# Attention maxima from columns to rows: four transposes per pair of heads, or a trip through DRAM

## The chip, the cores and the metric

The kernel runs on one NeuronCore of a Trainium2 chip. The metric is the device time of one execution in microseconds (us), as the median of several runs. One further execution was recorded by the hardware profiler; all readings of the profile come from it.

## The reference, cut to what matters

The input is `x` of shape (4, 128, 64, 64): four images, 128 channels, 4096 positions. A first layer is attention with four heads of 32 channels over the 4096 positions, followed by an output projection, the residual and a layer norm. A second layer adds a 3x3 convolution, a spectral branch and a selective scan (Mamba). The change is in the attention:

```python
Q = split_heads(x_flat @ Wq + bq)
K = split_heads(x_flat @ Wk + bk)
V = split_heads(x_flat @ Wv + bv)
attn = jax.nn.softmax(jnp.einsum('bhnd,bhmd->bhnm', Q, K) * scale, axis=-1)
out = jnp.einsum('bhnm,bhmd->bhnd', attn, V)
```

For each query the softmax takes off the largest of its 4096 scores before the exponential.

## The kernel before

**Halves and steps.** Queries are handled in chunks of 512 (`L`), and heads in pairs. A chunk with a pair is a "half", `H`; there are 32 chunks x 2 pairs = 64 halves. The keys of a half are walked through in 32 (`NT`) steps. A loop over a step counter `t` writes the whole program out in order, for all engines. In step `t` it issues

- `scores_for_exp` (L494): keys as weights, queries as the moving operand, so that the scores stand with keys on partitions and queries along the row. Each score is the sum of three matmuls per head: query high part, query low part (both against a K tile that holds high and low rows), and a matmul of `sel` with `MX[H]`, which subtracts the query's maximum. ScalarE then takes the exponential (L502).
- `scores_for_max` (L454), seven steps ahead (`LEAD = 7`) and for the half that comes next: here 128 queries are the weights and 512 keys move, so that queries stand on partitions. VectorE reduces them to a maximum for each query and block of keys (L461, tile `part`). The step number `s` gives the block of keys `m` and the group of queries `t`.
- `times_values` (L514): the exponentials of the step before, times the values, accumulated over the half.
- parts of the scan (L827 to L873) on ScalarE, VectorE and GpSimd, and one load of `bc` (L810) by SyncE's queue about every four steps.

The two heads of a pair lie on partitions 0 to 63 and 64 to 127, so their matmuls use the two halves of the array's rows and run as pairs.

**The other work** (projections, norm, convolution, gates, output, the chain for the maxima) is written as generators. A planner (`Plan`) resumes each once its time has come and the places that it asks for are free in this step: `"P"` TensorE, `"D"` VectorE, `"A"` ScalarE, `"B"` one of two PSUM banks, and `""` for nothing, which only ends the step. The order that results is fixed when the program is built; every engine and SyncE's DMA queue work through their instructions in that order and wait on semaphores.

**The maxima.** `maxima(H)` starts at `H * NT - LEAD`, when the last scores for maxima of that half are out. It reduces `part` to one maximum for each query and head (L467), splits the negative into a high and a low part (L469, L471), copies and writes them into two columns of each 64-wide half of the tile `wide` (L470, L471), has TensorE transpose `wide` in four pieces of 128 x 128 into a PSUM bank (L476), and has ScalarE copy the result to `MX[H]` (L482). There the maxima stand in rows 0 and 32 (`HD`) of each 64-row half, with the queries along the row; all other rows are zero. `wide` is zeroed once, at the start.

SyncE's queue also carries the K and V tiles (L385, L394), the queries (L434), the inputs (L336), and a chain through DRAM that normalises each half (`zd` L541, `zc` L546, `rd` L551, `rz` L554).

Of the kernel before, what the change touches and what calls it, by code (L numbers as in the profile page):

```python
# [9 lines left out]
F32 = mybir.dt.float32  # L10
F32R = mybir.dt.float32r
AF = mybir.ActivationFunctionType
ALU = mybir.AluOpType
AX = mybir.AxisListType
# [3 lines left out]
P = 128  # L18
W = 64
HEADS = 4  # L20
HD = P // HEADS
PAIRS = HEADS // 2
HS = P // 2
L = 512
RPC = L // W
TPC = L // P
# [135 lines left out]
def attention_then_conv_mamba(  # L162
# [17 lines left out]
    nc = tc.nc  # L180
    ctx.enter_context(tc.manual_schedule())
    B, C, N = x.shape
    NCH = N // L
# [5 lines left out]
    const = ctx.enter_context(tc.tile_pool(name="const", bufs=1))  # L189
    att = ctx.enter_context(tc.tile_pool(name="att", bufs=2))  # L190
    loc = ctx.enter_context(tc.tile_pool(name="loc", bufs=2))
    dram = ctx.enter_context(tc.tile_pool(name="dram", bufs=2, space=DRAM))
# [8 lines left out]
    for h in range(HEADS):  # L201
        k, j = divmod(h, 2)
# [3 lines left out]
    for h in range(HEADS):  # L206
        k, j = divmod(h, 2)
# [9 lines left out]
    for h in range(HEADS):  # L217
        k, j = divmod(h, 2)
# [39 lines left out]
    ident = cst[:, K_ID : K_ID + P]  # L258
# [57 lines left out]
    ]  # L316
    VA = [const.tile([P, TPC, HEADS, HD + 1], F32, name=f"V_{i}") for i in range(NCH)]

    wide = const.tile([P, TPC, 2, HS], F32, name="wide")
    nc.gpsimd.memset(wide, 0.0)  # L320
    state = const.tile([P, NH * NS], F32, name="state")
    carry = const.tile([P, NH, TAPS - 1], F32, name="carry")

    rows = [slice(j * HS, (j + 1) * HS) for j in range(2)]
    used = [slice(j * HS, j * HS + HD + 1) for j in range(2)]

    plan = Plan(2, {"x": 2, "f": 1})

    def bank_tile(bank, shape, name):
        return psum.tile(shape, F32, tag=f"m{bank}", name=name)  # L330
# [66 lines left out]
    QT, MX = {}, {}  # L397
# [42 lines left out]
    part = {}  # L440

    def scores_for_max(H, s):

        k = H % PAIRS
        m, t = divmod(s, TPC)
        assert have["K", k, m] == H // PAIRS // NCH
        if s == 0:
            part[H] = att.tile([P, TPC, 2, NCH], F32, tag="part", name=f"part_{H}")

        tag = "s2" if H == 0 and s % 2 else "s1"  # L450
        sc = psum.tile([P, 2, L], F32, tag=tag, name=f"s1_{H}_{s}")
        for n in range(2):
            for j in range(2):
                nc.tensor.matmul(  # L454
                    sc[:, j, :],
                    QT[H][rows[j], n, t * P : (t + 1) * P],
                    KK[k][m][rows[j], :],
                    start=n == 0,
                    stop=n == 1,
                )  # L460
        nc.vector.tensor_reduce(part[H][:, t, :, m], sc, AX.X, ALU.max)  # L461

    def maxima(H):

        yield "D"
        mx = att.tile([P, TPC, 2], F32, tag="mx", name=f"mx_{H}")
        nc.vector.tensor_reduce(mx, part.pop(H), AX.X, ALU.max)  # L467
        hi = att.tile([P, TPC, 2], F32R, tag="mhi", name=f"mhi_{H}")
        nc.vector.tensor_scalar(hi, mx, -1.0, None, ALU.mult)  # L469
        nc.vector.tensor_copy(wide[:, :, :, 0], hi)  # L470
        nc.vector.scalar_tensor_tensor(wide[:, :, :, HD], mx, -1.0, hi, ALU.mult, ALU.subtract)  # L471
        yield ""
        bank = yield "PB"
        pm = bank_tile(bank, [P, L], f"pm_{H}")
        for t in range(TPC):
            nc.tensor.transpose(  # L476
                pm[:, t * P : (t + 1) * P], wide[:, t].rearrange("p j d -> p (j d)"), ident
            )
        yield "A"
        plan.release(bank)  # L480
        MX[H] = att.tile([P, L], F32R, tag="MX", name=f"MX_{H}")
        nc.scalar.activation(MX[H], pm, AF.Copy)  # L482

    es, po, oz = {}, {}, {}

# [555 lines left out]
    for H in range(HALVES):  # L1041
        if H % PAIRS == 0:
            plan.at((H - 1) * NT - LEAD - 30, 0, load_q(H // PAIRS))
            plan.at((H - 1) * NT - LEAD - 22, 0, project_q(H // PAIRS))
        plan.at((H - 1) * NT - LEAD - 8, 0, place_q(H))
        plan.at(H * NT - LEAD, 0, maxima(H))
        plan.at((H + 1) * NT + 1, 0, normalise(H, (H + 1) * NT + 12))
# [11 lines left out]
    t = 6 - SLOT  # L1059
    loaded = 0  # L1060
    end = (CHUNKS + 3) * SLOT
    while t < end or not plan.idle():
        H, m = divmod(t, NT)
# [3 lines left out]
        if 0 <= h1 + 1 < HALVES:  # L1067
            scores_for_max(h1 + 1, s1)
        H, m = divmod(t - 1, NT)
# [114 lines left out]
```

## Time and profile before

| what | us |
|---|---|
| median of three runs (6036.54 to 6038.84) | 6037.3 |
| the profiled execution, its own time | 6038.33 |
| its span, first to last instruction | 6036.5 |
| TensorE matmuls busy | 5847.1 |
| VectorE busy | 4360.0 |
| ScalarE busy | 3586.6 |
| GpSimd busy | 4482.6 |
| first scores for maxima | 63.2 |
| last exponential scores | 5813 |

In the lines of the profile, PE is TensorE, PEld its weight loads (they may overlap matmuls), DVE VectorE, ACT ScalarE, POOL GpSimd, and SP or SPq SyncE and its queue of DMAs. L454 is line 454 of the kernel before. A group's line has the engine, the operation, the tiles (`out<-in`), the shapes and the count; then the busy time and the mean duration in ns; then the time that the engine sat idle ahead of such instructions, and what ended it. TensorE's matmuls are pipelined, so durations overlap: the distance between the starts of two groups says what the first one cost.

### The profile page before, as it was taken

The numbers are of one execution on the slowest core, as the hardware profiler recorded it, in microseconds if no ns is written. First come the engines' busy times: TensorE is split into PE (matmuls) and PEld (weight loads), VectorE is DVE, ScalarE is ACT, GpSimd is POOL, SyncE is SP. The second block draws the span as 40 slices with busy tenths as digits, with TensorE's granted clock in tenths as the row PEclk, the third lists the DMA queues.
The fourth block names the chain that finished last, engine by engine and source line by source line (L and its number), as shares of the span: only waits on it lengthen the run. The fifth ranks groups of instructions, "written<-read, shape, count | busy, mean of one in ns | idle before, by whom it ended". The sixth has DMA issues, their size and how long they took to land. (4 is left out here: it accounts for less than half of the span.)

```text
span 6036.5 us, 82731 instructions
## 1 busy us (share of the span) xinstructions
PE 5847.1 (97%) x31382; PEld 2443.1 (40%) x31382; DVE 4360.0 (72%) x4569; ACT 3586.6 (59%) x4826; POOL 4482.6 (74%) x4522
## 2 busy tenths in 40 slices
PE   5999999999999999999999999999999999999976
PEld 2444444444444444444444444444444444444422
DVE  4557777777777777777777777777777777777657
ACT  1455666666666666666666666666666666666653
POOL 0006888778887778888788888777888887888877
PEclk7999999999999999999999999999999999999988
DMA  4012222224333223223432222322433222222233
GB/s 125 25 36 58 65 71 75 71 70 110 82 89 73 73 72 74 72 64 89 104 84 82 74 68 71 75 68 73 108 75 92 67 67 63 66 71 63 62 98 89
DMA packets 266641, 455.28 MB, mean 75 GB/s; under 512 B 46688, under 2 KB 48256, under 8 KB 266240
## 3 DMA queue, kind: packets, MB, share of 16 engines
q1 hardware_dynamic: 261584, 448.11, 28.1%
q8 instruction: 246, 4.03, 0.3%
q10 hardware_dynamic: 4656, 1.87, 0.1%
q14 instruction: 155, 1.27, 0.1%
HBM read 375.68 MB, written 65.80 MB: 73 GB/s over the span
## 5 line engine op out<-in xcount | busy, mean ns | idle before, releaser
L461 DVE TENSOR_REDUCE part<-s 128x2 f32<-128x1024 f32 x2048 | 2498.1, 1221 | 1411.4 <-PE s L454 1407.6
L502 ACT ACTIVATE e<-s 128x1024 f32<-128x1024 f32 x2048 | 2095.5, 1023 | 2121.6 <-PE s L494 2117.0
L514 PE MATMUL po<-e,V 128*33 128x512 f32 x8192 | 2180.9, 605 | 2.4 <-DVE oz L525 0.3
L494 PE MATMUL s<-Q,K 64*128 64x512 f32 x8192 | 1501.0, 444 | 13.5 <-ACT e L502 10.2
L454 PE MATMUL s<-K,Q 64*128 64x512 f32 x8192 | 1308.9, 397 | 41.4 <-DVE part L461 32.3
L854 POOL TENSOR_TENSOR hs<-hs,bc 128x512 f32<-128x512 f32 x948 | 1211.0, 1277 | 170.3 <-DVE hs L844 101.3
L494 PEld LDWEIGHTS s<-Q,K 64*128 64x128 f32 x8192 | 610.2, 185 | 1736.3 <-ACT e L502 1237.0
L832 POOL TENSOR_TENSOR db<-u,bc 128x512 f32<-128x512 f32 x948 | 1215.6, 1282 | 0.0
L873 POOL TENSOR_TENSOR acc<-acc,hs 128x512 f32<-128x512 f32 x894 | 1145.4, 1281 | 70.1
L844 DVE TENSOR_TENSOR_SCAN hs<-dA,state,db 128x512 f32<-128x512 f32 x826 | 1052.8, 1275 | 41.9 <-ACT dA L827 40.1
L454 PEld LDWEIGHTS s<-K,Q 64*128 64x128 f32 x8192 | 750.1, 185 | 294.9 <-DVE part L461 129.4
L494 PE MATMUL s<-MX,sel 64*128 64x512 f32 x4096 | 808.0, 391 | 0.0
L827 ACT ACTIVATE dA<-dt,negA 128x512 f32<-128x512 f32 x1024 | 703.2, 687 | 115.7 <-DVE V L844 69.5
L853 POOL COPY state<-hs 128x1 f32<-128x1 f32 x858 | 157.9, 184 | 789.8 <-DVE hs L844 786.0
L514 PEld LDWEIGHTS po<-e,V 128*33 128x33 f32 x8192 | 305.4, 109 | 886.5 <-issue 840.8
L494 PEld LDWEIGHTS s<-MX,sel 64*128 64x128 f32 x4096 | 383.9, 185 | 90.7
L928 PE MATMUL pf<-xp,cw 128*128 128x512 f32 x576 | 288.2, 618 | 0.0
L558 POOL TENSOR_TENSOR op<-op,rz 128x512 f32<-128x512 f32 x32 | 41.4, 1294 | 178.6 <-DMA rz<-rd 175.8
L844 DVE TENSOR_TENSOR_SCAN hs<-dA,zero,db 128x512 f32<-128x512 f32 x128 | 163.2, 1275 | 0.9 <-POOL db L832 0.7
L880 PE MATMUL acc<-V,cst 128*128 128x512 f32 x140 | 95.0, 783 | 63.6 <-POOL V L854 63.5
L928 PEld LDWEIGHTS pf<-xp,cw 128*128 128x128 f32 x576 | 96.8, 189 | 119.6 <-issue 117.9
L712 POOL TENSOR_TENSOR xs<-xs,sg_x 128x512 f32<-128x512 f32 x64 | 81.8, 1279 | 79.3 <-ACT sg_x L636 79.3
(147 smaller groups left out, 3571.2 us busy)
## 6 DMA issues: line engine op xcount, KB each, us to landing
bc<-bcd SPq DMA_DIRECT2D x487, 512.0 KB
Q<-qd SPq DMA_DIRECT2D x256, 128.0 KB
K<-kd SPq DMA_DIRECT2D x64, 256.0 KB
K<-bcd SPq DMA_DIRECT2D x42, 256.0 KB
vd<-vst SPq DMA_DIRECT2D x32, 264.0 KB
V<-vd SPq DMA_DIRECT2D x32, 264.0 KB
xq<-in_x SPq DMA_DIRECT2D x32, 256.0 KB
xk<-in_x SPq DMA_DIRECT2D x32, 256.0 KB
```

The costliest lines, as they stand in the source:

```text
L454: nc.tensor.matmul(sc[:, j, :], QT[H][rows[j], n, t * P : (t + 1) * P], KK[k][m][rows[j], :], start=n == 0, stop=n == 1,)
L461: nc.vector.tensor_reduce(part[H][:, t, :, m], sc, AX.X, ALU.max)
L494: nc.tensor.matmul(s[:, j, :], sel[rows[j], :] if n == 2 else KK[k][i][rows[j], t * P : (t + 1) * P], mov[rows[j], :], start=n == 0, stop= ...
L502: nc.scalar.activation(e, s, AF.Exp)
L514: nc.tensor.matmul(po[H][used[j], :], VA[i][:, t, 2 * k + j, :], e[:, j, :], start=m == 0, stop=m == NT - 1,)
L827: nc.scalar.activation(dA[c, v], dts[c][hf], AF.Exp, scale=negA[:, k : k + 1])
L832: engine.tensor_tensor(db[c, v], us[c][hf], bcs[c, n][0], ALU.mult)
L844: nc.vector.tensor_tensor_scan(hs, dA.pop((c, v)), db.pop((c, v)), state[:, k : k + 1] if c % NCH else zero, ALU.mult, ALU.add,)
L853: nc.gpsimd.tensor_copy(state[:, k : k + 1], hs[:, L - 1 :])
L854: nc.gpsimd.tensor_tensor(hs, hs, bcs[c, n][1], ALU.mult)
L873: nc.gpsimd.tensor_tensor(accs[c, hf], accs[c, hf], hs, ALU.add)
L928: nc.tensor.matmul(pf, cw[:, k, :], xps[c][:, dy : dy + RPC, dx : dx + W], start=k == 0, stop=False)
```

## The change

The maxima reach `MX[H]` by way of DRAM. VectorE writes both parts into one tile `neg` with 16 words on each partition: part, head, and four query groups. One DMA stores it to a DRAM tile `md`. In the next step four DMAs load it back, one for each head and part, each into one row of 512 words. The transposes, the PSUM bank, the copy to `wide` and ScalarE's eviction are gone. `MX[H]` is now one of two tiles that are zeroed once and used in turn.

For the row to be in the order of the queries, and for the loads to have runs of more than one word, the groups of queries in `scores_for_max` change: group `t` takes queries `t, t+4, t+8, ...` instead of 128 successive ones. Partition `p` then has the maxima of queries `4p` to `4p+3`, and a row load reads 128 runs of four words. So the weights at this place are read from the query tile at every fourth word.

```diff
-    wide = const.tile([P, TPC, 2, HS], F32, name="wide")
-    nc.gpsimd.memset(wide, 0.0)
+    max_rows = [const.tile([P, L], F32R, name=f"MX_{k}") for k in range(2)]
+    for k in range(2):
+        nc.gpsimd.memset(max_rows[k].bitcast(F32), 0.0)
...
     def scores_for_max(H, s):
...
-            part[H] = att.tile([P, TPC, 2, NCH], F32, tag="part", name=f"part_{H}")
+            part[H] = att.tile([P, 2, TPC, NCH], F32, tag="part", name=f"part_{H}")
...
                 nc.tensor.matmul(
                     sc[:, j, :],
-                    QT[H][rows[j], n, t * P : (t + 1) * P],
+                    QT[H][rows[j], n, t::TPC],
                     KK[k][m][rows[j], :],
...
-        nc.vector.tensor_reduce(part[H][:, t, :, m], sc, AX.X, ALU.max)
+        nc.vector.tensor_reduce(part[H][:, :, t, m], sc, AX.X, ALU.max)

     def maxima(H):

         yield "D"
-        mx = att.tile([P, TPC, 2], F32, tag="mx", name=f"mx_{H}")
+        mx = att.tile([P, 2, TPC], F32, tag="mx", name=f"mx_{H}")
         nc.vector.tensor_reduce(mx, part.pop(H), AX.X, ALU.max)
-        hi = att.tile([P, TPC, 2], F32R, tag="mhi", name=f"mhi_{H}")
-        nc.vector.tensor_scalar(hi, mx, -1.0, None, ALU.mult)
-        nc.vector.tensor_copy(wide[:, :, :, 0], hi)
-        nc.vector.scalar_tensor_tensor(wide[:, :, :, HD], mx, -1.0, hi, ALU.mult, ALU.subtract)
-        yield ""
-        bank = yield "PB"
-        pm = bank_tile(bank, [P, L], f"pm_{H}")
-        for t in range(TPC):
-            nc.tensor.transpose(
-                pm[:, t * P : (t + 1) * P], wide[:, t].rearrange("p j d -> p (j d)"), ident
-            )
-        yield "A"
-        plan.release(bank)
-        MX[H] = att.tile([P, L], F32R, tag="MX", name=f"MX_{H}")
-        nc.scalar.activation(MX[H], pm, AF.Copy)
+        neg = att.tile([P, 2, 2, TPC], F32R, tag="mhi", name=f"neg_{H}")
+        nc.vector.tensor_scalar(neg[:, 0], mx, -1.0, None, ALU.mult)
+        nc.vector.scalar_tensor_tensor(neg[:, 1], mx, -1.0, neg[:, 0], ALU.mult, ALU.subtract)
+        yield ""
+        md = dram.tile([P, 2, 2, TPC], F32, tag="md", name=f"md_{H}")
+        nc.sync.dma_start(md, neg.bitcast(F32))
+        yield ""
+        MX[H] = max_rows[H % 2]
+        for j in range(2):
+            for r in range(2):
+                row = j * HS + r * HD
+                nc.sync.dma_start(
+                    MX[H][row : row + 1, :].bitcast(F32).rearrange("o (p t) -> o p t", p=P),
+                    md[:, r : r + 1, j, :].rearrange("p o t -> o p t"),
+                )
```

## The prediction, made before the changed kernel was run

> **What bounds the kernel now.** I read four views in this order: the busy table by windows, the costliest groups, the timeline around one set of transposes, and SyncE's part of the timeline. The windows come first because the page's averages mix three stages. The columns are TensorE, its weight load, VectorE, ScalarE, GpSimd, then granted clock, DMA share and GB/s:
>
> ```profile
> PE 5847.1 (97%) x31382; PEld 2443.1 (40%) x31382; DVE 4360.0 (72%) x4569; ACT 3586.6 (59%) x4826; POOL 4482.6 (74%) x4522
> ...
> 500.00:3000.00 2500.00, 2483.22 (x13540) 1041.91 (x13538) 1860.02 (x1938) 1554.63 (x2100) 2003.07 (x2030) 1.00 0.30 78
> ...
> 5813.00:6036.00 223.00, 142.64 (x262) 48.93 (x258) 169.94 (x188) 86.38 (x142) 168.37 (x156) 0.80 0.34 100
> ```
>
> In the long middle TensorE is busy 2483 of 2500 us at full clock; VectorE (74%), ScalarE (62%) and GpSimd (80%) all have air. From about 130 us to 5813 us the time is a sum of TensorE work: whatever TensorE sheds there comes off the end, unless something new makes it wait. The first 130 us wait for loads and VectorE, the last 223 us for the scans on VectorE and GpSimd; the change touches neither.
>
> Next, the groups that the change touches:
>
> ```profile
> L494 PE MATMUL s<-Q,K 64*128 64x512 f32 x8192 | 1501.0, 444 | 13.5 <-ACT e L502 10.2
> L454 PE MATMUL s<-K,Q 64*128 64x512 f32 x8192 | 1308.9, 397 | 41.4 <-DVE part L461 32.3
> ...
> L454 PEld LDWEIGHTS s<-K,Q 64*128 64x128 f32 x8192 | 750.1, 185 | 294.9 <-DVE part L461 129.4 <-issue 1.5
> ...
> L494 PE MATMUL s<-MX,sel 64*128 64x512 f32 x4096 | 808.0, 391 | 0.0
> ```
>
> The mean durations tell how much of a weight load shows. An MX matmul, whose weights were loaded under the matmul before it, lasts 391 ns. Of the L494 Q,K matmuls the first pair of each step follows a full-array matmul and has to wait for its weights; that lifts the mean to 444, so one exposed load is 2 x (444 - 391) = 106 ns. At L454 the mean is 397, 6 ns over 391: 8192 x 6 / 2 (two matmuls of a pair run at once) is about 25 us of exposed loads in all, in the some 200 steps where L454 waited for VectorE and couldn't load early. Elsewhere its loads are hidden, and the timeline shows under what:
>
> ```profile
> 2865.14 0.40 PE L494 MATMUL s<-MX,sel 64*128 64x512 f32 x2
> 2865.14 0.42 PEld L454 LDWEIGHTS s<-K,Q 64*128 64x128 f32 x4
> 2865.37 0.63 PE L454 MATMUL s<-K,Q 64*128 64x512 f32 x4
> ...
> 2865.93 0.66 PE L476 MATMUL pm<-cst,wide 128*128 128x128 f32 x4
> ...
> 2866.52 1.05 PE L514 MATMUL po<-e,V 128*33 128x512 f32 x4
> ```
>
> L454's loads start with the MX pair, 0.23 us before L454's first matmuls. So a load of 0.106 us has 0.23 us of cover. A step with nothing else in it takes 2.34 us (L454 at 3005.71 and next at 3008.05). The transposes take 2866.52 - 2865.93 = 0.59 us of TensorE for each of the 64 halves.
>
> [...] here SyncE waited 104.3 us for 64 small stores (rd, L554), 1.63 us each, 4.0 at most. I use the trace's numbers.
>
> **The change part by part.**
>
> (1) Transposes gone. 256 transposes leave TensorE, four for each half. In the timeline, their slot is 0.59 us where the value matmul follows (53 halves) and 0.39 us where another full-array matmul follows (10 halves); the remaining one lies in the prologue, where TensorE isn't the bound. The step from L454 into the slot (2865.37 to 2865.93) costs the same whatever comes next. 53 x 0.59 + 10 x 0.39 = **-35 us**.
>
> (2) The eviction at L482 goes: 64 x 0.59 = 38 us of ScalarE. ScalarE isn't the bound; its lateness at L494 is 10.2 us in all. I count 0, at most -5. On VectorE the copy at L470 goes (64 x 0.31 = 20 us); the tensor_scalar and the scalar_tensor_tensor stay with as many elements. TensorE lost 32.3 us to late VectorE work at L454, mostly in other places than the maxima: 0 to -5, I take 0. The PSUM bank and the ScalarE slot let other small jobs move by a step or so; they are the same instructions, +-3.
>
> (3) L454's weights now step 16 bytes[...]. At no penalty: 0. At half rate [...] a load takes 213 ns, still inside the 230 ns of cover with 17 to spare, and only the already exposed loads of the PE-bound part grow: some 150 x 0.107 = +16 us. Above 2.15 times, every load sticks out: 2 pairs x 2016 steps, +4.0 us for each ns beyond 230. At a quarter of the rate (427 ns): 197 x 4.03 = +794 us. [...] I take 0, and keep +16 inside the likeliest case.
>
> (4) The new path. SyncE gets 5 DMAs for each half, 320 in all, 64 x (0.33 + 4 x 0.36) = 113 us of issue, plus 64 waits of about 1.6 us for the store to land before the first row load. SyncE waits 3532 us for GpSimd before the bc loads at L810, so it has this time; what stands behind is listed now. For odd halves, SyncE near half 31 looks like this:
>
> ```profile
> 2862.01 0.37 SPq L810 DMA_DIRECT2D bc<-bcd  x1
> 2862.47 0.42 SPq L1004 DMA_DIRECT2D out<-ob  x1
> 2862.99 0.38 SPq L385 DMA_DIRECT2D K<-kd  x1
> 2873.01 0.37 SPq L810 DMA_DIRECT2D bc<-bcd  x1
> ```
>
> VectorE finishes the negated maxima at 2863.40 here (L471), and the first MX matmul of the half starts at 2874.67: 11.3 us. The new chain: store issue 0.35, landing 1.63, four row loads at 0.36 each 1.45, landing 1.63, in sum 5.1 us; with the longest landing seen twice, 9.8 us. Both fit, and SyncE is free until 2873.01. In even halves the row loads stand behind a bc load that waits for GpSimd (in half 32 until 2950.84); rows issued by 2952.7 and landed by 2954.3 to 2956.7 against a first use at 2964.4. Behind them the load of xq and the K and V loads slip by 1.5 us; xq is used eight steps later (19 us at least). bc follows a release by GpSimd that comes later still. So: 0. If that cover were gone, each us of lateness would cost TensorE one us for each half.
>
> (5) The packets: 64 x (128 + 512) runs of 64 and 16 bytes, at the 9 ns of a 32-byte packet in this trace some 370 us spread over 16 engines, 23 us each, at a DMA share of 0.30: 0. The waits of TensorE for four loads instead of one ScalarE result are executed by its sequencer, which runs ahead of the array (the semaphore instruction for a matmul stands about 1 us before it in the trace): 0.
>
> **Sum.** 0 - 35 + 0 + 0: the profiled execution of 6038.3 us (span 6036.5 and 1.8 around it), 1.0 above the median of 6037.3, becomes 6003; against the median **6002 us**. Own range of this case: 5990 (-35 with -12 from VectorE, ScalarE and shifts) to 6025 (+16 for the loads and some shifts).
>
> **Rivals.**
> - *Weight loads stick out.* The 16-byte step slows the load by more than 2.15 times. For it: [...] the cover is only 2.15 loads. [...] It decides from 9 ns beyond the cover (9 x 4.0 = 36 eats the gain). At 2.4 times (256 ns): +105 - 35, 6107 us; at 3 times (320 ns) 6365; at 4 times 6796. Slower.
> - *Maxima arrive late.* The DRAM chain of odd halves takes more than 11.3 us, because the row loads queue behind a 512 KB bc load or because 128 runs of 16 bytes into one partition land slowly. At 15 us: 31 x 3.7 = +115 - 35, 6117 us. Against: twice the longest landing seen still fits.
> - *The gain turns into another wait.* With 35 us less on TensorE, VectorE or GpSimd runs late instead. GpSimd at 80% speaks against it. It would give between 6025 and 6049, that is, no change.
>
> **How the numbers follow.** A run of this kernel tells about 0.2% (12 us) from no change. Hidden loads and timely maxima: 0.72, all of it faster. Weight loads stick out: 0.17, of which 0.02 end within 0.2% and 0.02 below 6090. Late maxima: 0.05, 0.01 of it within 0.2%. Another wait: 0.05, split between faster (0.01) and no change (0.04). The last 0.01 is that the new order helps by more. That makes faster 0.74, same 0.07, slower 0.19. The range starts at 5990; to hold eight in ten it passes the likeliest case's 6025, takes in no change (0.07) and small exposures (up to 22 ns beyond the cover), 6090.
>
> **What would show it.** In the groups after: no L476 and L482; LDWEIGHTS of the scores for maxima at 185 ns (no penalty) or near 290 (half rate), and its matmul's mean near 397 (right) or far above, with steps of 2.34 us growing (wrong). On the path: no wait of TensorE for MX loads. SyncE: waits for md near 64 x 1.6 us. If the steps in the middle stay at 2.34 us and the span falls by other than about 35 us, term (1) or (4) is wrong.

## The result: 7.7 us faster, where 35 were forecast

| kernel | median us | lowest to highest | ratio to before |
|---|---|---|---|
| before (20 runs) | 6039.11 | 6036.54 to 6042.3 | |
| after (20 runs) | 6031.4 | 6027.62 to 6035.37 | 0.9986 [0.998, 0.9993] |

The changed kernel is faster by 7.7 us, 0.14%. The direction was right, but only about a fifth of the gain arrived. By the prediction's own measure (a difference under 0.2%, 12 us, is no change) this is the case to which it gave a chance of 0.07. The time is beyond its likeliest case (to 6025 us), and it lies inside the wide range only because that was stretched to 6090 to take in no change and small exposures. The profiled execution of after took 6027.62 us (span 6025.8) and was its fastest run, so lines of its page are read for durations and waits, and totals are read from medians.

The busy table of after, and the window of the long middle with the same columns as for before:

```profile
PE 5844.9 (97%) x31126; PEld 2786.9 (46%) x31126; DVE 4307.5 (71%) x4505; ACT 3548.3 (59%) x4762; POOL 4486.9 (74%) x4523
...
500.00:3000.00 2500.00, 2487.84 (x13470) 1194.78 (x13468) 1839.18 (x1915) 1540.82 (x2076) 2011.84 (x2037) 1.00 0.29 78
```

TensorE is still the bound: 2487.84 of 2500 us at full clock. 256 matmuls are gone (31382 to 31126), yet its busy time has hardly moved. What has moved is PEld, the weight loads: 2443.1 to 2786.9 us, 344 us more with fewer loads. The groups say which load:

```profile
L496 PE MATMUL s<-Q,K 64*128 64x512 f32 x8192 | 1504.1, 445 | 7.8 <-ACT e L504 4.3
L456 PE MATMUL s<-K,Q 64*128 64x512 f32 x8192 | 1338.7, 404 | 37.9 <-DVE part L463 33.9
...
L456 PEld LDWEIGHTS s<-K,Q 64*128 64x128 f32 x8192 | 1122.5, 308 | 191.9 <-DVE part L463 98.9
...
L496 PE MATMUL s<-MX,sel 64*128 64x512 f32 x4096 | 820.9, 396 | 0.0
...
L496 PEld LDWEIGHTS s<-MX,sel 64*128 64x128 f32 x4096 | 384.3, 185 | 92.2 <-DMA MX<-md 0.4
```

Three things are to be seen. The load at L456, whose weights now step 16 bytes, is recorded with 308 ns where L454 had 185; the loads at L496 are as they were at L494 (185). The matmuls at L456 went from 397 to 404 ns, and those with MX, during which the slow loads run, from 391 to 396. (The two matmuls of a pair start together: 3 ns apart at the median at L454 and at L456, where one lasts 393 ns at the median.) And the waits are nearly as before: the weight loads of the MX matmuls waited once, 0.4 us, for rows of MX in the whole run, the matmuls never; the wait for ScalarE at L496 fell from 10.2 to 4.3 us; that for VectorE stayed (32.3, now 33.9).

**Where 308 ns of load go.** First a step of after in which the load could start early (timeline of TensorE and its loads; start, duration):

```profile
3007.53 0.40 PE L496 MATMUL s<-MX,sel 64*128 64x512 f32 x2
3007.53 0.55 PEld L456 LDWEIGHTS s<-K,Q 64*128 64x128 f32 x4
3007.77 0.64 PE L456 MATMUL s<-K,Q 64*128 64x512 f32 x4
...
3010.12 0.63 PE L456 MATMUL s<-K,Q 64*128 64x512 f32 x4
...
3012.48 0.40 PE L456 MATMUL s<-K,Q 64*128 64x512 f32 x2
```

The load starts with the MX pair and L456's first pair starts 0.24 us later, as before (0.23). From L456 to the next it is 2.35 and 2.36 us, where before had 2.34. Over all plain steps after 200 us (steps with nothing in them but the matmuls of values, of Q and K, and of MX) the median of this distance is 2.344 us in before and 2.357 in after; the 2.340 and 2.354 that the expectations below name are nearer to the fastest steps. The load grew by 123 ns (308 - 185) and the plain step by 13, so most of it is still covered. Now a step in which L456 waited for VectorE, so that its load stands bare; before first, then after:

```profile
3022.92 0.30 PEld L454 LDWEIGHTS s<-K,Q 64*128 64x128 f32 x4 [0.51 <-DVE part L461]
3022.92 0.74 PE L454 MATMUL s<-K,Q 64*128 64x512 f32 x4
...
3023.59 0.15 PEld L514 LDWEIGHTS po<-e,V 128*33 128x33 f32 x4 [0.37 <-issue]
```

```profile
3015.04 0.54 PEld L456 LDWEIGHTS s<-K,Q 64*128 64x128 f32 x4 [0.48 <-DVE part L463]
3015.04 0.86 PE L456 MATMUL s<-K,Q 64*128 64x512 f32 x4
...
3015.83 0.15 PEld L516 LDWEIGHTS po<-e,V 128*33 128x33 f32 x4 [0.25 <-issue]
```

From L454's start to the next load it was 0.67 us, and is 0.79: 0.12 us more, the amount by which the record of a load grew (308 - 185). So the visible part of a load, which the prediction worked out as 106 ns, is now, by the same estimate, 106 + 123 = 229 ns. That is 1 ns less than its cover of 230 (2865.37 - 2865.14 in before). The steps whose load is fully bare say the same: from their first pair of scores for maxima to the second it is 340 ns in before and 463 in after (medians).

Over the steps after 200 us I added up, in the traces, the distance between the two pairs of the scores for maxima. It is 474.1 us in before and 500.5 in after: +26.4 us. With the transposes' -35 this leaves -8.6; the measured difference is -7.7.

**The new path on SyncE** (timeline of SyncE's queue near half 31, then the largest of its waits: what for, us in total, times, longest):

```profile
2855.05 0.37 SPq L812 DMA_DIRECT2D bc<-bcd  x1
...
2856.05 0.35 SPq L475 DMA_DIRECT2D md<-neg  x1
2856.51 0.42 SPq L386 DMA_DIRECT2D K<-kd  x1
2861.27 2.45 SPq L481 DMA_DIRECT2D MX<-md  x4
```

```profile
SPq L812 <- POOL hs L856: 3173.1, 473, 25.0
...
SPq L481 <- DMA md<-neg: 120.7, 34, 4.5
```

The store is issued by 2856.40 and the first row load at 2861.27. Over odd halves the median of this gap is 4.2 us: the store stands behind a 512 KB load of `bc`, whose packets began at 2856.1, while the store's 128 packets of 64 bytes ran only from 2859.2 to 2860.6. The four row loads take 2.45 us of issue, near 0.6 each; their last packet ended at 2864.84. The first MX matmul of the half came at 2867.46, 2.6 us later. All of it stays under cover: SyncE waits 3173 us for GpSimd anyway.

### The profile page after: what moved, and what is told of

Read it like the earlier page. It is cut to its first block, busy times and chain, and to the rows that moved or that the text cites. A ratio compares the mean times of both kernels' runs of the same rounds, so it can differ in the third digit from the quotient of the medians.

```text
span 6025.8 us, 82754 instructions
## 1 busy us (share of the span) xinstructions
PE 5844.9 (97%) x31126; PEld 2786.9 (46%) x31126; DVE 4307.5 (71%) x4505; ACT 3548.3 (59%) x4762; POOL 4486.9 (74%) x4523
## 5 line engine op out<-in xcount | busy, mean ns | idle before, releaser
L516 PE MATMUL po<-e,V 128*33 128x512 f32 x8192 | 2180.9, 605 | 2.3 <-DVE oz L527 0.3
L496 PE MATMUL s<-Q,K 64*128 64x512 f32 x8192 | 1504.1, 445 | 7.8 <-ACT e L504 4.3
L496 PEld LDWEIGHTS s<-Q,K 64*128 64x128 f32 x8192 | 610.4, 185 | 1727.4 <-ACT e L504 1253.2
L456 PE MATMUL s<-K,Q 64*128 64x512 f32 x8192 | 1338.7, 404 | 37.9 <-DVE part L463 33.9
L456 PEld LDWEIGHTS s<-K,Q 64*128 64x128 f32 x8192 | 1122.5, 308 | 191.9 <-DVE part L463 98.9
L496 PE MATMUL s<-MX,sel 64*128 64x512 f32 x4096 | 820.9, 396 | 0.0
L516 PEld LDWEIGHTS po<-e,V 128*33 128x33 f32 x8192 | 305.3, 109 | 733.0 <-issue 694.5
L496 PEld LDWEIGHTS s<-MX,sel 64*128 64x128 f32 x4096 | 384.3, 185 | 92.2 <-DMA MX<-md 0.4
```

The lines of the kernel that those rows point to most:

```text
L456: nc.tensor.matmul(sc[:, j, :], QT[H][rows[j], n, t::TPC], KK[k][m][rows[j], :], start=n == 0, stop=n == 1,)
L496: nc.tensor.matmul(s[:, j, :], sel[rows[j], :] if n == 2 else KK[k][i][rows[j], t * P : (t + 1) * P], mov[rows[j], :], start=n == 0, stop= ...
L516: nc.tensor.matmul(po[H][used[j], :], VA[i][:, t, 2 * k + j, :], e[:, j, :], start=m == 0, stop=m == NT - 1,)
```

## The experiments

Two readings had to be told apart. **The theory of the slow load**: the transposes' 35 us did come off, and the slow stepped load took 27 back. **The rival**: the gain is lost on the way of the maxima (DRAM, late arrival). The kernels compared below ran beside the kernel before; ratios are to it.

### e1: after, with contiguous weights

```diff
-                    QT[H][rows[j], n, t::TPC],
+                    QT[H][rows[j], n, t * P : (t + 1) * P],
...
-    MX[H][row : row + 1, :].bitcast(F32).rearrange("o (p t) -> o p t", p=P),
-    md[:, r : r + 1, j, :].rearrange("p o t -> o p t"),
+    MX[H][row : row + 1, :].bitcast(F32).rearrange("o (t p) -> o t p", p=P),
+    md[:, r : r + 1, j, :].rearrange("p o t -> o t p"),
```

> The changed kernel with its trip through DRAM, but with the weights of the scores for maxima read contiguously again (128 successive queries), so the four row loads are made of 512 runs of one word. Theory (the 16-byte step of the weights eats the gain): weight loads at L456 back to 184 ns, plain steps back to 2.340 us, the whole -35 us of the transposes appears: 6002 to 6006 us, ratio 0.9940 to 0.9950. Rival (the trip through DRAM, with its waits on SyncE's queue and the new order of small jobs, eats it): about as the changed kernel, ratio 0.9986, or slower because of four times as many runs. Rival (the transposes were worth only 8 us): ratio 0.9986, with steps of 2.340 us.

Measured: 6172.72 us, ratio 1.0219 [1.0205, 1.0233], far from the 6002 to 6006 us of the theory of the slow load; only the rival's "or slower because of four times as many runs" fits it. The loads did recover (187 ns, a plain step 2.347 us at the median). But every row load now has 512 runs of one word, and its issue takes 1.03 us at the median instead of 0.58. TensorE's waits (us in total, times, longest) and one of them in the timeline:

```profile
PE s L496 <- DMA MX<-md: 107.7, 54, 4.2
```

```profile
2920.37 0.47 PE L496 MATMUL s<-MX,sel 64*128 64x512 f32 x1 [1.75 <-DMA MX<-md]
2923.90 0.76 PE L496 MATMUL s<-MX,sel 64*128 64x512 f32 x1 [3.06 <-DMA MX<-md]
2923.90 1.61 PE L456 MATMUL s<-K,Q 64*128 64x512 f32 x4
2925.44 1.92 PE L516 MATMUL po<-e,V 128*33 128x512 f32 x4
...
2929.28 1.05 PE L516 MATMUL po<-e,V 128*33 128x512 f32 x4
```

This is the rival "Maxima arrive late", made real. Here more was lost than the waits alone. In the windows after it (the third number from the end is the granted clock) TensorE is busy throughout, but at half its clock for about 4 us:

```profile
2924.00:2926.00 2.00, 2.00 (x7) 0.92 (x9) 0.45 (x1) 1.02 (x1) 0.00 (x0) 0.50 0.13 45
2926.00:2928.00 2.00, 2.00 (x8) 0.61 (x6) 0.78 (x1) 0.59 (x2) 0.00 (x0) 0.50 0.00 0
2928.00:2932.00 4.00, 4.00 (x26) 1.79 (x24) 3.93 (x5) 3.73 (x8) 1.73 (x3) 0.92 0.16 35
```

In this stretch L516 takes 1.92 us, and 1.05 in the next step. It is not the only one: between 200 and 5900 us the granted clock of e1 fell to half 28 times, for 3.4 or 6.8 us, 154 us in all, and in before and after not once between 200 and 5700 us. Against the best kernel below (6003.5), the 108 us of waits came to 169 us. The run mixes two effects, so it settles neither reading by itself.

### e2: before, with the stepped weights alone

The transposes stay. ScalarE's copy writes the maxima in the order of the queries, so that the row is the same as in before.

```diff
-                    QT[H][rows[j], n, t * P : (t + 1) * P],
+                    QT[H][rows[j], n, t::TPC],
...
-        nc.scalar.activation(MX[H], pm, AF.Copy)
+        nc.scalar.activation(
+            MX[H].rearrange("q (p t) -> q t p", t=TPC), pm.rearrange("q (t p) -> q t p", p=P), AF.Copy
+        )
```

> The kernel before with nothing changed but the weights of the scores for maxima, which take every fourth query; ScalarE writes the transposed maxima back into the order of the queries. Transposes stay, no trip through DRAM. Theory: weight loads at L454 306 ns, plain steps 2.354 us, +25 to +30 us, ratio 1.0041 to 1.0050. Rival (the step costs nothing, the DRAM path does): ratio 1.000.

Measured: 6066.75 against 6040.19, ratio 1.0045 [1.0032, 1.0057], +26.6 us. Its group of loads:

```profile
L454 PEld LDWEIGHTS s<-K,Q 64*128 64x128 f32 x8192 | 1112.0, 307 | 202.8 <-DVE part L461 109.4 <-issue 1.7
```

The step alone costs 26.6 us, with no DMA in the matter. The copy itself got slower (1.10 us instead of 0.59), but TensorE's waits for ScalarE at the scores didn't grow (5.5 us, in before 10.2). The distance between the two pairs sums to 501.1 us, +27.0 against before: the whole loss lies at this place. Compared step by step, some 20 us of it lie in the 196 steps whose load is wholly or in part bare in one of the two kernels, and the other 7 are 4 ns in each of 1784 covered steps.

### e3, e8, e4: other steps

```diff
-                    QT[H][rows[j], n, t::TPC],
+                    QT[H][rows[j], n, t // 2 * 2 * P + t % 2 : (t // 2 + 1) * 2 * P : 2],   # e3, 8 bytes
+                    QT[H][rows[j], n, t : t + 3 * P : 3],                                 # e8, 12 bytes
+                    QT[H].rearrange("p n l -> p (n l)")[rows[j], t : 1024 : 8],           # e4, 32 bytes
```

e3's row loads take 256 runs of two words each; e8 and e4 leave the row loads as in after.

The expectations speak of 16-byte lines. There a line is a 16-byte stretch of a row, and their number is counted over the 128 words of a load. That the time goes with this count was my assumption; the runs show how long a load takes at each step.

> The changed kernel with weights that step two words (8 bytes) instead of four[...]; row loads of 256 runs of two words. Theory (what counts is the number of lines per weight): no more than one line for two weights, loads at 184 ns, plain steps 2.340 us, ratio 0.9940 to 0.9950 as with contiguous weights. Rival (any step slows the load): loads between 184 and 306 ns and part of the gain gone, ratio 0.996 to 0.9986.

> The changed kernel with weights that step three words (12 bytes); the queries of the groups overlap and one quarter is left out, so the maxima are not those of all queries and only the time counts. Theory (a line for each weight at 16 bytes, one for two at 8 bytes; here three lines for four weights): loads between those of two words (193 ns) and of four (306 ns), near 270 ns if the time goes with the number of lines, plain steps 2.345 us or less since the load stays under its cover. Rival (what counts is whether a step stays below 16 bytes): loads of about 190 ns as with two words.

> The changed kernel with weights that step eight words (32 bytes), through the high and the low part of the query tile; the maxima are therefore those of other query words and the softmax is shifted wrongly, only the time counts. Theory (one line for each weight, no matter which): loads at 306 ns as with four words, plain steps 2.354 us. Rival (the cost grows with the distance, as if whole stretches were read through): loads well above 306 ns, steps well above 2.354 us, span above 6400 us.

Their groups of loads at L456, in the order e3, e8, e4:

```profile
L456 PEld LDWEIGHTS s<-K,Q 64*128 64x128 f32 x8192 | 782.5, 193 | 285.5 <-DVE part L463 128.7 <-issue 1.7
```

```profile
L456 PEld LDWEIGHTS s<-K,Q 64*128 64x128 f32 x8192 | 986.5, 250 | 204.4 <-DVE part L463 114.7 <-DVE klo L357 1.5 <-issue 1.5
```

```profile
L456 PEld LDWEIGHTS s<-K,Q 64*128 64x128 f32 x8192 | 1160.0, 321 | 187.8 <-DVE part L463 97.0 <-issue 1.7
```

| step, bytes | 16-byte stretches, by count | record, ns | load (record - 78), ns | bare step, ns | plain step, us | time, us |
|---|---|---|---|---|---|---|
| 4 (before) | 32 | 184 to 185 | 106 | 340 | 2.344 | |
| 8 (e3) | 64 | 193 | 115 | 347 | 2.351 | 6011.02, ratio 0.9953 [0.994, 0.9967] |
| 12 (e8) | 96 | 250 | 172 | 406 | 2.352 | 6019.18 (single run) |
| 16 (after) | 128 | 307 to 308 | 229 | 463 | 2.357 | 6031.4 |
| 32 (e4) | 128 | 321 | 243 | 468 | 2.373 | 6055.13 (single run) |

78 is the part of a record before that didn't show (184 - 106). A bare step is the median from the first to the second pair of scores for maxima where the load is fully bare; it needs no such part taken off, and it grows over before by 7, 66, 123 and 128 ns, the records by 9, 66, 123 and 137. Among these five steps the load time goes with the count of 16-byte stretches from 64 on, at about 1.8 ns each (115, 172, 229 ns for 64, 96, 128), and none took less than 106 ns. From 16 to 32 bytes the distance doubles, the count doesn't, and the load goes from 229 ns only to 243 by the records, 234 by the bare steps: the count fits the times, the distance doesn't. None of the three expectations was met to the number: e3 lies between its theory and its rival, e8's load is shorter than the 270 ns named, and e4's plain steps grew where none was expected to.

With e4 the load, 243 ns by the same estimate, sticks out past its cover of 230. The prediction's formula gives two times 13 ns in a step; against after the plain step grew by 16. In time, the 57 ns from 12 to 16 bytes cost 12 us, and the next 5 to 14 ns cost 24 (e8 and e4 are single runs). So the cliff shows in these runs, right beside the step that the change uses.

e3 is faster than after by 20 us. It also had two late arrivals of MX, 3.2 us in all: with 256 runs in each row load the cover of 11.3 us is nearly used up, and with the 512 of e1 it is not enough.

### e5 and e7: contiguous weights with two more steps of lead, and its control

e5 gives e1 more time: LEAD 9, with the start moved two steps earlier. e7 is after with that same edit.

```diff
-    LEAD = 7
+    LEAD = 9
...
-            plan.at(... if b else 6 - SLOT + i, 0, project_kv(b, i))
+            plan.at(... if b else 4 - SLOT + i, 0, project_kv(b, i))
...
-    t = 6 - SLOT
+    t = 4 - SLOT
```

> Contiguous weights and row loads of 512 runs of one word as in the first experiment, but the scores for maxima run nine steps ahead instead of seven (LEAD = 9, and the program starts two steps earlier), so that the chain through DRAM has some 5 us more. Theory (contiguous weights give back the whole value of the transposes, and what the first experiment lost was only the lateness of its row loads): the 107.7 us of TensorE waiting for MX loads vanish, plain steps 2.340 us, 6002 to 6010 us, ratio 0.994 to 0.995; two more steps of filling at the start may cost up to 4 us. Rival (the many one-word runs slow the kernel in other ways, on the DMA queues or SyncE): above 6060 us although no wait for MX is left.

> The changed kernel with LEAD = 9 and nothing else, as the control for the experiment on lateness. Theory (the changed kernel has no lateness of the maxima to lose, only slow weight loads): as the changed kernel, 6029 to 6036 us, ratio 0.998 to 0.9995, with loads of 306 ns and plain steps of 2.354 us. Rival (hidden lateness of the maxima costs part of the gain): 6010 to 6020 us.

Measured: e5 6024.89, ratio 0.9975 [0.9966, 0.9985], with no wait for MX at all and loads of 185 ns. e7 6055.23, ratio 1.0025 [1.0015, 1.0035]. They missed the upper end of what was expected by 15 and 19 us. The longer lead was not free here: it cost 6055.2 - 6031.4 = 23.8 us from after to e7. In the traces the first MX matmul comes 8.8 us later (138.2 against 129.4 us). TensorE also waits 6.8 us, in three places, for K loads that are in time in after; around two of these waits the granted clock fell to half, for 6.8 and 3.4 us. The rest I didn't split. Between e5 and e7 only the step and the shape of the row loads differ: 30.3 us in favour of contiguous. That is about the size that e2 gave.

### e6: contiguous, with the sorting done by the store

The store writes 2048 single words in the order of rows, and one DMA loads all four rows.

```diff
-        nc.sync.dma_start(md, neg.bitcast(F32))
+        nc.sync.dma_start(
+            md.rearrange("q p -> p q"), neg.bitcast(F32).rearrange("p j r t -> p (j r t)")
+        )
...
+        nc.sync.dma_start(
+            MX[H][::HD, :].bitcast(F32), md.rearrange("(q t) p -> q (t p)", t=TPC)
+        )
```

> Contiguous weights, LEAD = 7; the turn from columns to rows is made by the store: 2048 runs of one word go to DRAM in the order of the rows, and a single load of four rows of 2 KB fills MX. Two DMAs for each half instead of five. Theory: the chain gets shorter (one load to issue, no 16-byte runs into one partition), no wait for MX on TensorE, loads 184 ns, plain steps 2.340 us, 6000 to 6006 us, ratio 0.9935 to 0.9948. Rival (2048 single words take long, in issue or in landing): the first use in odd halves comes before the rows, some us of wait in each of 32 halves, 6040 us or more.

```profile
PE s L496 <- DMA MX<-md: 106.0, 32, 6.2
```

Measured: 6153.83, ratio 1.0186 [1.0172, 1.02], late in 32 halves: the rival came true. From the end of the store's issue to the row load it took 12.2 us at the median, where after has 4.2. Sorting word by word was too slow here on either side of the trip.

### e9, e10, e11: without DRAM

All three copy the columns of `neg` straight into the rows of `MX`, with no store and no wait for it: e9 contiguous with 16 DMAs of 128 single words, e10 at 8 bytes with 8 DMAs of 128 x 2 words, e11 at after's 16 bytes with 4 DMAs of 128 x 4 words.

```diff
-        md = dram.tile([P, 2, 2, TPC], F32, tag="md", name=f"md_{H}")
-        nc.sync.dma_start(md, neg.bitcast(F32))
-        yield ""
         MX[H] = max_rows[H % 2]
-        for j in range(2):
-            for r in range(2):
-                row = j * HS + r * HD
-                nc.sync.dma_start(
...
+        for b in range(2):                                   # e10
+            for j in range(2):
+                for r in range(2):
+                    row = j * HS + r * HD
+                    nc.sync.dma_start(
+                        MX[H][row : row + 1, b * 2 * P : (b + 1) * 2 * P].bitcast(F32),
+                        neg[:, r, j, 2 * b : 2 * b + 2].bitcast(F32),
+                    )
```

> Contiguous weights, LEAD = 7, and no DRAM: sixteen DMAs for each half go straight from the columns of neg into the rows of MX, each with one group of 128 queries (128 single words). Theory: weight loads 184 ns, plain steps 2.340 us; no store to wait for, so even sixteen issues of some 0.4 us and a landing of 2 us (8 to 9 us) come before the first use in odd halves (11.3 us): 6003 to 6008 us, ratio 0.994 to 0.995. Rival (single words are slow also between SBUF partitions, as the 512-run loads from DRAM were): waits for MX on TensorE, above 6050 us.

> Weights that step two words, no DRAM: eight DMAs for each half straight from neg into MX, each with 128 runs of two words. Theory: weight loads 193 ns as in the kernel with a step of two, no wait for MX, 6006 to 6011 us, ratio 0.9945 to 0.9955. Rival (what the step of two lost against contiguous weights was the two late arrivals of 3.2 us, not the loads): 6002 to 6005 us.

> The changed kernel with its weights at every fourth word, but four DMAs straight from neg into MX instead of the trip through DRAM. Theory (the trip is hidden and costs nothing, the stepped weights cost all of it): as the changed kernel, 6029 to 6034 us, ratio 0.998 to 0.9993, loads 306 ns, steps 2.354 us. Rival (the trip through DRAM costs something that no wait shows): 6015 us or less.

**e9** took 6026.36, ratio 0.9978 [0.9971, 0.9986], where 6003 to 6008 were expected. The loads are 186 ns, but 16 issues at 0.6 us fill SyncE's queue (timeline near half 31) and the last ones come late (waits of TensorE):

```profile
2851.55 10.62 SPq L479 DMA_DIRECT2D MX<-neg  x16
```

```profile
PE s L494 <- DMA MX<-neg: 8.8, 13, 2.0
```

That is less than half of the 20.7 us by which the profiled execution of e9 is longer than that of e10. Where the rest went stays open.

**e11** took 6031.47, ratio 0.9988 [0.9981, 0.9994]: the same as after (6031.4). The trip through DRAM costs nothing that can be told apart, and the rival falls.

**e10** took 6003.5 (6002.53 to 6007.67), ratio 0.9942 [0.993, 0.9955], 35.4 us under the 6038.87 of before. It is the fastest of all the kernels here, before and after included. The time is in the range of the rival stated for it (6002 to 6005), not of its theory (6006 to 6011): what e3 lost was not the loads, though its waits for MX are only 3.2 of the 7.5 us between the two. The trace agrees on the loads: a bare step is 7 ns longer than in before, which over some 155 bare steps is about 1 us. Its groups and the window of the middle:

```profile
L456 PE MATMUL s<-K,Q 64*128 64x512 f32 x8192 | 1315.6, 398 | 41.3 <-DVE part L463 36.7
...
L456 PEld LDWEIGHTS s<-K,Q 64*128 64x128 f32 x8192 | 781.1, 193 | 286.5 <-DVE part L463 127.5
```

```profile
500.00:3000.00 2500.00, 2487.25 (x13532) 1049.92 (x13530) 1845.14 (x1922) 1548.40 (x2080) 2016.89 (x2045) 1.00 0.30 79
```

It executes as many matmuls as after, but in the same 2500 us it gets through 13532 of them instead of 13470, with the same busy time. That is 0.46%, or 26 us over the 5690 us of the PE-bound part. The medians of e10 and e11, which differ in the step of the weights and in the split of the copies that goes with it, are 28.0 us apart. TensorE has no wait for MX.

## Why the prediction was right or wrong, by its steps

- **Term (1), transposes gone, -35: right.** e2 has the step with the transposes: +26.6. After has the step without them: -7.7. The difference is -34.3. e10, with no transposes and a step that costs about 1 us, gained 35.4. (The ten shorter slots are 0.49 us in the trace of before, not 0.39: one us.)
- **Term (2), counted as 0 with small shifts: right in size.** The wait for ScalarE at L496 fell by 5.9 us (10.2 to 4.3), that for VectorE rose by 1.6. The first is a little more than the 5 that was allowed for the eviction, the second is small.
- **Term (3), the step of the weights, taken as 0: this is the step that failed.** It was worth +27 (-7.7 where the other terms leave -35, and +26.6 alone in e2). The prediction held the outline in hand: at half rate only the bare loads grow, "some 150 x 0.107 = +16", kept at the edge of the likeliest case. But its centre was put at no penalty, and the trace of before, whose loads at L454 and L494 take 128 words in a row (185 ns each), prices no stepped load: no penalty and half rate were both my assumptions. The half-rate variant too was sized low twice. A load grew by 123 ns, not by the 107 assumed, and the cover had 1 ns to spare, not 17, so that the covered steps lost some ns each as well. 20 + 7, as in e2, is the sum that should have stood there.
- **The price of a load, 106 ns**, worked out from before, holds for contiguous weights (records of 187 ns in e1, 185 in e5 and 186 in e9, where before has 185) and for those at 8 bytes nearly (115). At 16 bytes it is 229.
- **Term (4), the new path, 0: right in effect, mis-sized inside.** Landing of the store 4.2 us in odd halves instead of 1.63 (the `bc` load ahead of it), row loads 0.58 instead of 0.36. From the store's issue to the last packet of the rows it is 2864.84 - 2856.05 = 8.8 us of the 11.3. The stated worst case of 9.8 covered it. e1 and e6 show that the rival was close: with 512 runs in each load, or a scattered store, it came true.
- **Term (5), packets and semaphores, 0: right as far as the runs tell.** e11 with no store took the same time, and e10, whose MX tile is filled by eight loads, still gained all of term (1).
- **Rivals.** "Weight loads stick out" stayed under its threshold of 230 ns by 1 ns, and yet the covered steps lost some ns; e4 crossed it. The prediction thought that 17 ns were to spare there, at an estimated 4 us for each ns beyond; by that estimate it hung on the last one that the change came out faster at all, and that is luck. "The gain turns into another wait" forecast a time of 6025 to 6049, and the measured one lies there by coincidence: the gain went into loads that fill TensorE, not into a wait.

What stays open: e2, e5 against e7 and e10 against e11 give 26.6, 30.3 and 28.0 us for the step. Their intervals overlap, and I can't say whether the differences mean anything. The shares of bare and covered loads are counts from one trace each. Why a covered step loses a few ns to a load of 229 ns under a cover of 230 is not shown either.

## What to carry to other kernels

The hidden weight load here had as much cover as the work ahead of it, one pair of matmuls and 230 ns, so ask of every change in an access pattern how much of the cover it uses, and count apart the loads that stand bare: here those paid in full, 123 ns in a step. When a layout is changed to make a transfer cheaper, look for the smallest step that still suffices: here 8 bytes gave the same freedom as 16 at almost no price (7 ns in a bare step, where 16 bytes took 123). Where the trace has no example of the access that a change brings in, "free" is an assumption too: measure that access alone, as e2 did, before the centre of the forecast rests on it.

## What the runs showed of the hardware that was not expected

- The weight load of 128 fp32 columns took, by the estimate above, 106 ns contiguous and 115, 172 and 229 ns at steps of 8, 12 and 16 bytes (records of 185, 193, 250 and 308 ns). A step of 32 bytes cost little more than one of 16 (234 to 243 ns). A count of 16-byte stretches, about 1.8 ns each from 64 on, fits the steps of 8, 12 and 16 bytes, and within 5 to 14 ns that of 32; what in the hardware makes it so is not shown.
- SyncE's issue of a row load grew with its runs: 0.58 us for 128 runs into one row, 0.94 for 256 and 1.03 for 512 (medians); the store of 128 x 64 bytes took 0.34. A store of 2048 single words to DRAM took 12.2 us until its load could be issued.
- After TensorE had waited twice in e1 (1.75 and 3.06 us), its granted clock was 0.50 for about 4 us; 28 such stretches made 154 us of the run. In e7 6.8 us at half clock went with one wait of 2.9 us. The 107.7 us of waits in e1 stood beside a loss of 169 us against e10; that the waits bring the lower clock about is not shown.
- In e10 a DMA laid words of 128 partitions straight into a row of one partition; 8 such copies took 5.06 us of SyncE's queue near half 31, and no MX matmul of that run waited for them.
